# Splitting a 514-column product over two PSUM banks: 512 and 2 columns where there were two times 257

## The chip, the cores and the metric

The kernel runs on one core of one Trainium2 chip. A core has five engines that run side by side and meet at semaphores: TensorE (matmuls, out of SBUF into PSUM; the profile shows the matmuls as PE and the loads of their stationary operand as PEld), VectorE (DVE), ScalarE (ACT), GpSimd (POOL, here mostly the issue of indirect transfers) and SyncE (SP, the issue of the plain ones). The metric is the device time of one execution in microseconds. A float32 bank of PSUM holds 512 columns on each of 128 partitions in this kernel, so 514 columns need two banks.

## What is computed

The input `x` is (32, 512, 1024): a batch, 512 channels, 1024 nodes. Two layers, each with a residual and a layer norm over the last axis:

```python
# layer 0: attention over the nodes, in each batch
q = einsum('c,bcn->bn', wq, x);  k = einsum('c,bcn->bn', wk, x)
scores = q[:, None, :] + k[:, :, None]
scores = where(scores > 0, scores, 0.01 * scores)
att = softmax(scores, axis=-1)
agg = einsum('bcn,bmn->bcm', x, att)
x = layernorm(x + relu(einsum('oc,bcm->bom', adj, agg) + bm[None, :, None]))
# layer 1: a product with the elementwise square of adj
x = layernorm(x + einsum('bnf,nm->bmf', x, adj * adj) + bias)
```

The score of a pair depends on a sum q + k alone, through a function with one bend at zero. Once the nodes are sorted by q, the nodes on either side of the bend are a head and a tail of the sorted list, so the softmax's sums over 1024 nodes become two running sums, one from each end, each with its own exponential weight.

## The kernel before

**Data of a batch.** `adj @ x` comes first (`product`, L306 to L313): for each of 8 groups of 128 nodes four float32 matmuls of 128x128 weights by 512 columns, into one PSUM bank `z_ps`, copied to SBUF by ScalarE (`zt`, L316). Each node's row has 514 columns: 512 products, a one (whose running sum gives the softmax's denominator), and the node's own q. GpSimd scatters the rows in the order of q to DRAM (`scatter`, L324), and SyncE loads them back so that each of 128 partitions holds 8 neighbours of the sorted list (`sums_load`, L343).

**Running sums and carries.** VectorE runs along the 8 rows of every partition, upwards (`up`, L353) and downwards (`down`, L366), each step a scaled add of 514 or 513 columns. What a partition still lacks is the sum over all partitions before it (for the upward sums) or behind it (for the downward ones): the carry. It is a matmul of the partition totals, 128 partitions by 514 columns, with a triangle of ones, `before` or `behind` (`carry`, L374 to L382). As 514 columns don't fit one bank, the carry is two matmuls into two tiles of 257 columns, taken from the pool `p1` of four banks under the tag `m`, which the carries share with `z_ps`, `sum_ps`, `qk_ps` and `qk_tp`. `carry_copy` (L384 to L387) has ScalarE copy both tiles to SBUF: the upward carry into row 0 of the table, the downward one to a tile of its own. VectorE adds the carry to all rows (`spread_carry`, L402 to L405), and SyncE writes the table to DRAM.

**The rest of layer 0.** GpSimd gathers from the table one row for every node (`gather`, L432), ScalarE and VectorE mix the two halves with the exponential weights (`mix_scale` L454, `mix` L459), TensorE transposes the mix back to channels by nodes (`turn`, L482, eight 128-column transposes for each of four tiles of channels), VectorE adds the residual (L490), and ScalarE does statistics and norm.

**Layer 1.** The product with adj * adj is done by a Strassen-like scheme of quarters (`U`, `V`, `Y`, `Z`, `C11` and others; L540 and L575), seven products where eight would be plain, each of 512-column matmuls, preceded in places by a short bfloat16 matmul that brings the bias (L538).

**Order.** The order is written out by hand, as words of the form operation.batch.index: `head` for the first batches, `loop` once for each of the batches 12 to 25, `tail` for the last. Each engine executes its own share of that list in order. A round of the loop works on up to six batches in different stages: it loads one, ranks another, does sums and carries of a third, gathers and mixes a fourth, and so on. Around the carries a round reads

```
mx.-3.3 cu.-2 zc.-1.2 d.-2.5 s1.-4.2 t.-3.1 ... uc.-2
tu.-2.1 rt.-3 st.-4.3 cd.-2 z.-1.6 dc.-2 rce.-3 zc.-1.5 td.-2.0
```

`cu` and `cd` are the matmuls of the upward and the downward carry, `uc` and `dc` their copies, `t` the transposes, `tu` and `td` VectorE's adds of the carries, `rt` ScalarE's square root. On TensorE, `cu` stands ahead of a `t` and `cd` ahead of a `z`.

Of the kernel before, what the change touches and what calls it, by code (L numbers as in the profile page):

```python
# [34 lines left out]
F32 = mybir.dt.float32  # L35
# [7 lines left out]
P = 128  # L43
# [6 lines left out]
def adj_resnorm_kernel(  # L50
# [10 lines left out]
    nc = tc.nc  # L61
    B, C, N = x.shape
# [5 lines left out]
    ZR = C + 2  # L68
# [10 lines left out]
    p1 = ctx.enter_context(tc.tile_pool(name="p1", bufs=4, space=bass.MemoryType.PSUM))  # L79
# [21 lines left out]
    for h in range(2):  # L101
# [7 lines left out]
    before = const.tile([P, P], F32, name="before")  # L109
    nc.vector.memset(before, 1.0)  # L110
    nc.gpsimd.affine_select(
        before, before, pattern=[[1, P]], compare_op=ALU.is_gt, fill=0.0, base=0,
# [260 lines left out]

    def carry(b, m, v):  # L374

        half = ZR // 2
        ps = []
        for h in range(2):
            t = p1.tile([P, C], F32, tag="m", name=f"carry_ps_{b}_{h}_{m is before}")[:, 0:half]
            nc.tensor.matmul(t, m, v[:, h * half : (h + 1) * half], start=True, stop=True)  # L380
            ps.append(t)
        return ps  # L382

    def carry_copy(ps, to):  # L384
        half = ZR // 2
        for h, t in enumerate(ps):
            nc.scalar.copy(to[:, h * half : (h + 1) * half], t)  # L387

    def carry_up(b):
        st[b].cup = carry(b, before, st[b].end)  # L390

    def carry_up_copy(b):
        carry_copy(st[b].cup, st[b].tab[:, 0, 0:ZR])

    def carry_down(b):
        st[b].cdown = carry(b, behind, st[b].zs[:, 0, :])

    def carry_down_copy(b):
        st[b].carry = one.tile([P, ZR], F32, tag="carry", name=f"carry_{b}")
        carry_copy(st[b].cdown, st[b].carry)  # L400
# [562 lines left out]
```

## Time and profile before

| | before |
|---|---|
| median of three runs | 2062.61 us (2061.65 to 2064.26) |
| the profiled execution, in all | 2065.32 us |
| its span, first to last instruction | 2063.6 us |
| mean granted TensorE clock | 0.991 |
| TensorE busy, matmuls | 2004.7 us (97%), 6609 records |
| TensorE busy, weight loads | 956.7 us (46%), 6609 records |
| VectorE busy | 1674.9 us (81%) |
| ScalarE busy | 1496.3 us (73%) |
| GpSimd busy | 874.6 us (42%) |
| DMA | 541 MB, mean 262 GB/s |

A float32 matmul of the program shows up as two MATMUL records and two LDWEIGHTS records. In a row of groups, "x128" counts records, the first number after the bar is the time in which any of them ran, the second the mean length of one. Consecutive records overlap, since a matmul's way through the array is longer than the time for which it takes the input. Where a row says "idle", it is the idle time of that engine just before these instructions, and behind the arrow stands what ended it; "issue" means that nothing seen in the trace held it.

### The profile page before, as it was taken

Reading aid. Unit: us, or ns where it says so; the run is one execution under the profiler, and the core shown is the slowest. Engines: PE = TensorE matmul, PEld = TensorE weight load, DVE = VectorE, ACT = ScalarE, POOL = GpSimd, SP = SyncE. Lnnn points to the kernel's source line nnn. Section 1 sums busy time; section 2 is a strip of 40 time slices with the busy share of each in tenths; the row PEclk is TensorE's granted clock in tenths of the full one; section 3 lists DMA queues with packets and bytes.
Section 4 is the critical chain, followed back from the end, with each engine's and each line's share of the span. In section 5 each row is a group of like instructions: output and inputs, shape, how many; then the busy total and the mean of one; then the engine's idle time right before and its main releaser. Section 6 shows DMA issues by size and latency. Waiting matters only on the chain. (4 is left out here: it accounts for less than half of the span.)

```text
span 2063.6 us, 22066 instructions
## 1 busy us (share of the span) xinstructions
PE 2004.7 (97%) x6609; PEld 956.7 (46%) x6609; DVE 1674.9 (81%) x2778; ACT 1496.3 (73%) x2560; POOL 874.6 (42%) x1106
## 2 busy tenths in 40 slices
PE   8999999999999999999999999999999999999976
PEld 4444444444444444444444544444444444444432
DVE  6888898798877889887889888789778888789672
ACT  3566787678776777777777777777777777767566
POOL 4344543344343444443444443453444443443421
PEclk9999999999999999999999999999999999999988
DMA  5558776866667766667766767766677766677752
GB/s 226 212 222 312 275 287 266 306 264 257 271 245 291 307 255 246 271 266 292 306 241 250 273 268 296 290 249 258 255 276 306 276 244 268 245 269 273 286 204 82
DMA packets 137967, 541.04 MB, mean 262 GB/s; under 512 B 14404, under 2 KB 14416, under 8 KB 129656
## 3 DMA queue, kind: packets, MB, share of 16 engines
q1 hardware_dynamic: 80464, 337.47, 41.2%
q0 software_dynamic: 57344, 202.15, 26.0%
q8 instruction: 52, 0.85, 0.2%
q14 instruction: 67, 0.55, 0.1%
q10 hardware_dynamic: 40, 0.02, 0.0%
HBM read 270.29 MB, written 269.29 MB: 261 GB/s over the span
## 5 line engine op out<-in xcount | busy, mean ns | idle before, releaser
L310 PE MATMUL z_ps<-adj_t,x 128*128 128x512 f32 x2048 | 906.6, 593 | 0.4 <-ACT zt L316 0.4
L310 PEld LDWEIGHTS z_ps<-adj_t,x 128*128 128x128 f32 x2048 | 384.1, 190 | 448.0 <-issue 439.5
L324 POOL DMA_INDIRECT sorted_z<-zt,to x256 | 377.2, 1473 | 481.0 <-ACT zt L316 403.7
L432 POOL DMA_INDIRECT got<-table,of x256 | 262.2, 1024 | 209.6 <-issue 87.8
L271 DVE SCALAR_TENSOR_TENSOR junk_v<-qb,qkc,tie 128x1024 uint8<-128x1024 f32 x256 | 328.2, 1282 | 4.0
L284 ACT ACTIVATE junk_s<-qb,qkc 128x1024 bf16<-128x1024 f32 x256 | 293.9, 1148 | 18.9 <-DVE qb L261 17.0
L475 POOL TENSOR_SCALAR var<-var 128x1 f32<-128x1 f32 x128 | 46.3, 362 | 461.9 <-ACT junk L468 458.6
L454 ACT ACTIVATE got<-got,w 128x512 f32<-128x512 f32 x256 | 172.2, 713 | 64.2 <-DVE w L449 56.6
L316 ACT COPY zt<-z_ps 128x512 f32<-128x512 f32 x256 | 144.4, 577 | 68.4 <-PE z_ps L310 63.2
L459 DVE SCALAR_TENSOR_TENSOR got<-got,w 128x512 f32<-128x512 f32 x256 | 180.9, 745 | 10.9 <-ACT got L454 10.7
L490 DVE SCALAR_TENSOR_TENSOR x<-agg_ps,nbm,x 128x1024 f32<-128x1024 f32 x128 | 161.4, 1280 | 23.1 <-PE agg_ps L482 22.7
L372 DVE SCALAR_TENSOR_TENSOR tab<-tab,ac 128x513 f32<-128x513 f32 x224 | 168.0, 750 | 3.0
L631 ACT ACTIVATE g<-g,nb,var 128x1024 f32<-128x1024 f32 x128 | 157.8, 1238 | 11.8 <-POOL nb L625 11.8
L468 ACT ACTIVATE junk<-g,tot 128x1024 bf16<-128x1024 f32 x128 | 146.6, 1146 | 21.3 <-DVE g L595 16.8
L362 DVE SCALAR_TENSOR_TENSOR tab<-tab,ac 128x514 f32<-128x514 f32 x192 | 144.5, 752 | 16.9 <-ACT ac L348 11.7
L468 ACT ACTIVATE junk<-x,tot 128x1024 bf16<-128x1024 f32 x128 | 146.8, 1147 | 13.6 <-DVE x L490 8.3
L405 DVE TENSOR_TENSOR tab<-tab,carry 128x2052 f32<-128x2052 f32 x64 | 144.8, 2292 | 11.5 <-ACT carry L387 11.5
L540 PE MATMUL sum_ps<-x,adj 128*128 128x512 f32 x256 | 131.4, 637 | 16.3 <-ACT x L508 16.3
L482 PE MATMUL agg_ps<-ident,got 128*128 128x128 f32 x1024 | 133.4, 278 | 11.2 <-issue 4.7
L508 ACT ACTIVATE x<-x,var 128x1024 f32<-128x1024 f32 x128 | 138.5, 1149 | 0.7 <-DVE var L504 0.6
L601 DVE SCALAR_TENSOR_TENSOR g<-sum_ps,g 128x512 f32<-128x512 f32 x64 | 44.0, 687 | 111.8 <-ACT junk_s L284 75.3
L482 PEld LDWEIGHTS agg_ps<-ident,got 128*128 128x128 f32 x1024 | 115.2, 143 | 36.3 <-DVE x L490 12.2
(121 smaller groups left out, 2698.8 us busy)
## 6 DMA issues: line engine op xcount, KB each, us to landing
table<-tab SPq DMA_DIRECT2D x64, 2056.0 KB
tab<-sorted_z SPq DMA_DIRECT2D x64, 1028.0 KB
x<-in_x_dram SPq DMA_DIRECT2D x128, 512.0 KB
out_dram<-g SPq DMA_DIRECT2D x128, 512.0 KB
sorted_z<-zt,to POOLq DMA_INDIRECT x256
got<-table,of POOLq DMA_INDIRECT x256
adj_in<-in_adj_dram SPq DMA_DIRECT2D x1, 1024.0 KB
table<-end SPq DMA_DIRECT2D x32, 2.0 KB
```

What stands on the lines that cost most here:

```text
L271: nc.vector.scalar_tensor_tensor(junk, s.qb, s.q[:, j : j + 1], tie[:, at : at + N], ALU.subtract, ALU.is_gt, accum_out=s.rank[:, j : j + 1],)
L284: nc.scalar.activation(junk, s.qb, AF.Sign, bias=s.k[:, j : j + 1], accum_out=s.sign[:, j : j + 1])
L310: nc.tensor.matmul(s.z[j], xt[:, c, j * P : (j + 1) * P], adj_t[:, c, :], start=(c == 0), stop=(c == CT - 1),)
L324: nc.gpsimd.indirect_dma_start(out=sorted_z[b % 2][:, :], out_offset=bass.IndirectOffsetOnAxis(ap=s.to[:, j : j + 1], axis=0), in_=zt[:, j ...
L372: nc.vector.scalar_tensor_tensor(v, v, c, s.zs[:, j + 1, 0:D], ALU.mult, ALU.add)
L432: nc.gpsimd.indirect_dma_start(out=s.got[:, j, :], out_offset=None, in_=table[b % 2][:, :], in_offset=bass.IndirectOffsetOnAxis(ap=s.of[:, ...
L454: nc.scalar.activation(down, down, AF.Copy, scale=s.w[:, 1, j : j + 1])
L459: nc.vector.scalar_tensor_tensor(up, up, s.w[:, 0, j : j + 1], down, ALU.mult, ALU.add)
L468: nc.scalar.activation(junk, t, AF.Square, bias=v[0][:, i : i + 1], scale=-float(N), accum_out=v[1][:, i : i + 1],)
L482: nc.tensor.transpose(s.agg[o][:, j * P : (j + 1) * P], s.got[:, j, o * P : (o + 1) * P], ident)
L490: nc.vector.scalar_tensor_tensor(t[:, o, :], s.agg[o], nbm[:, o : o + 1], t[:, o, :], ALU.max, ALU.add, accum_out=s.v0[0][:, o : o + 1],)
L631: nc.scalar.activation(g, g, AF.Identity, bias=s.nb[:, m : m + 1], scale=s.v1[1][:, m : m + 1])
```

## The change

The carry's 514 columns are split where the first bank is full. The first matmul takes columns 0 to 511, the second the last two: column 512, the one's running sum, and column 513, q, which the table doesn't use. The copies are split in the same places. Both tiles come from the same pool and tag as before, there are as many matmuls, copies and banks as before, and the order of the words is unchanged.

```diff
     def carry(b, m, v):
 
-        half = ZR // 2
         ps = []
-        for h in range(2):
-            t = p1.tile([P, C], F32, tag="m", name=f"carry_ps_{b}_{h}_{m is before}")[:, 0:half]
-            nc.tensor.matmul(t, m, v[:, h * half : (h + 1) * half], start=True, stop=True)
+        for h, (lo, hi) in enumerate(((0, C), (C, ZR))):
+            t = p1.tile([P, C], F32, tag="m", name=f"carry_ps_{b}_{h}_{m is before}")[:, 0 : hi - lo]
+            nc.tensor.matmul(t, m, v[:, lo:hi], start=True, stop=True)
             ps.append(t)
         return ps
 
     def carry_copy(ps, to):
-        half = ZR // 2
-        for h, t in enumerate(ps):
-            nc.scalar.copy(to[:, h * half : (h + 1) * half], t)
+        for (lo, hi), t in zip(((0, C), (C, ZR)), ps):
+            nc.scalar.copy(to[:, lo:hi], t)
```

Here `P` is 128, `C` is 512 and `ZR` is 514.

## The prediction

> **What bounds the kernel now.** I read the page's busy times and slices first, then busy time by stretch, then the groups with their shapes kept apart, then the waits of TensorE, and last single instructions around carries in the timeline.
>
> ```profile
> PE 2004.7 (97%) x6609; PEld 956.7 (46%) x6609; DVE 1674.9 (81%) x2778; ACT 1496.3 (73%) x2560; POOL 874.6 (42%) x1106
> ...
> PE   8999999999999999999999999999999999999976
> ```
>
> TensorE is busy 97% of the span; VectorE, second, 81%. The slices put the missing 3% at both ends. The table of stretches makes this sharper (stretch, its length, then busy time of PE, PEld, DVE, ACT, POOL with counts, granted clock, DMA share, GB/s):
>
> ```profile
> 100.00:600.00 500.00, 491.34 (x1592) 232.48 (x1591) 422.44 (x707) 371.69 (x645) 218.98 (x267) 1.00 0.72 277
> 600.00:1100.00 500.00, 498.76 (x1655) 238.95 (x1654) 414.02 (x689) 374.25 (x641) 219.28 (x272) 1.00 0.69 270
> 1100.00:1600.00 500.00, 497.62 (x1653) 238.52 (x1652) 417.33 (x694) 376.15 (x644) 219.70 (x272) 1.00 0.69 271
> 1600.00:1950.00 350.00, 347.08 (x1141) 165.87 (x1140) 287.61 (x466) 256.17 (x440) 149.54 (x192) 1.00 0.69 267
> ```
>
> Between 600 and 1600 us TensorE stands still for 3.6 us of 1000 (1.24 and 2.38), at full granted clock (1.00), while no other engine is above 84%. In the loop, what TensorE issues is the time; what the others do counts only when TensorE waits for it. Among its waits, this one recurs in the middle, TensorE's transposes waiting for VectorE's mix (us in total, times, longest):
>
> ```profile
> PE agg_ps L482 <- DVE got L459: 4.5, 9, 1.0
> ```
>
> I come back to it. The groups that the change touches, and the large products to compare with (count | busy us, mean ns of one | idle before):
>
> ```profile
> L310 PE MATMUL z_ps<-adj_t,x 128*128 128x512 f32 x2048 | 906.6, 593 | 0.4 <-ACT zt L316 0.4
> ...
> L380 PE MATMUL carry_ps_False<-tab,behind 128*128 128x257 f32 x128 | 34.0, 388 | 0.4 <-ACT tab L387 0.4
> ...
> L387 ACT COPY carry<-carry_ps_False 128x257 f32<-128x257 f32 x64 | 21.3, 368 | 7.8 <-PE carry_ps_False L380 7.3
> ```
>
> The trace has two MATMUL and two LDWEIGHTS records for each float32 product: 128 records a side are 64 matmuls, two carries in each of 32 batches. "Mean ns of one" holds the way through the array; the pace is busy over count: 906.6/2048 = 443 ns for 512 columns with the ends of runs in it, 427 to 430 between two starts. The same row shows that TensorE waits only 0.4 us in all for the release of a PSUM bank by the copy to zt. Here is one carry of the loop, and what surrounds it:
>
> ```profile
> 1114.27 1.03 PE L380 MATMUL carry_ps_False<-tab,behind 128*128 128x257 f32 x4
> ...
> 1115.14 1.88 PE L310 MATMUL z_ps<-adj_t,x 128*128 128x512 f32 x4
> ...
> 1115.54 0.63 ACT L387 COPY carry<-carry_ps_False 128x257 f32<-128x257 f32 x2
> 1115.57 0.19 PEld L310 LDWEIGHTS z_ps<-adj_t,x 128*128 128x128 f32 x1 [0.24 <-issue]
> ...
> 1116.20 2.29 DVE L405 TENSOR_TENSOR tab<-tab,carry 128x2052 f32<-128x2052 f32 x1 [0.36 <-ACT carry L387]
> ```
>
> Four 257-column records run from 1114.27 to the start of z_ps at 1115.14: 0.87 us, 217 ns each. The first 512-column record starts at 1115.14, and the weight load seen at 1115.57, with the second, 0.43 later; ahead of it the weight path was free for 0.24. So a record of N columns takes the array about N/1.2 ns (214, 427), and the load of 190 ns on the next record's weights starts with each matmul and is gone before that matmul has streamed. VectorE starts adding the carry at 1116.20, 0.03 us after the second copy ends (1115.54 + 0.63).
>
> What an *uncovered* load costs is seen where TensorE had stood still, a matmul, then loads:
>
> ```profile
> 1721.70 0.70 PE L310 MATMUL z_ps<-adj_t,x 128*128 128x512 f32 x1 [0.38 <-ACT zt L316]
> ```
>
> ```profile
> 1720.62 0.30 PEld L380 LDWEIGHTS carry_ps_True<-end,before 128*128 128x128 f32 x2 [0.69 <-ACT g L608]
> 1721.69 0.30 PEld L310 LDWEIGHTS z_ps<-adj_t,x 128*128 128x128 f32 x2 [0.78 <-ACT zt L316]
> ```
>
> The second load starts 0.11 us after the first (0.30 less one load's 0.19), and the 512-column matmul takes 0.70 instead of its usual 0.59. Ten such loads between 200 and 1960 us give 107 to 109 ns. That is how long an uncovered 128x128 float32 load holds the array, not its whole 190. For the transposes it is less:
>
> ```profile
> 1101.83 0.33 PE L482 MATMUL agg_ps<-ident,got 128*128 128x128 f32 x1 [0.42 <-DVE got L459]
> ```
>
> 0.33 against 0.273 for most of this line's matmuls: 57 ns.
>
> **What the Trainium skill says.** "TensorE: Matmul & The Clock Gate", section LDWEIGHTS, prices a weight load by columns, P/1.2: 107 ns for 128, as the 0.11 above. The same page's "Step-by-step" says that a load is pulled ahead of running matmuls into the background weight buffer; the trace agrees, and shows it one load ahead: each starts with the matmul before its own. "Wait — 56ns, not 53.3ns?" gives a floor of about 25 ns between matmul starts however few columns; no run here shows so small a matmul. "ScalarE: Activation LUTs", section What ACT_TABLE_LOAD costs, gives 186 ns + 0.833 ns per element for an ACTIVATE with immediate operands; the trace's copies have about that slope (577 for the 512 columns of L316, 369 for 257: 208/255 = 0.816) on a smaller base.
>
> **The change, part by part.**
>
> *TensorE.* Removed are four records of 257 columns, 4 x 217.5 = 870 ns. Added are two of 512, 2 x 429 = 858 ns, and two of 2 columns. The columns are the same 514, so streaming changes by nothing (2 columns stream in under 5 ns), but the number of weight loads stays four, and what covers them goes. The load of the first small record hides under the second large one. The load of the second small record can start only with the first small record, and has nothing over it: 107 ns, which also swallows the 25 ns floor. The load of whatever comes next starts with the second small record: 107 ns before a float32 matmul, 58 before a transpose. So
> - before a product: 858 + 107 + 107 - 870 = +202 ns; this is the neighbour of 31 carries (30 z_ps, one sum_ps);
> - before a transpose (L482 27 times, L252 four, L236 once): 858 + 107 + 58 - 870 = +153 ns, 32 carries;
> - once the bias matmul L538 follows, whose own load was uncovered anyway: about +100 ns.
>
> 31 x 0.202 + 32 x 0.153 + 0.1 = 11.3 us of TensorE work. The small records aren't in this trace: below, 58 for each of the two loads (58 + 58 - 12 = 104 ns a carry, 6.7 us); above, the load's full 190 (368 ns, 23.6 us). I take 107, which is measured on this very kind of load, and keep both ends.
>
> *What absorbs some.* Where TensorE waits soon after a carry, the wait shrinks. By the timeline 14 of the 64 carries have such a wait within some 4 us behind them (the nine before L482, five others before 420 and after 1700 us): 14 x 0.16 = -2.2 us. Most of the loop's carries have none.
>
> *ScalarE.* Two copies of 257 (353 and 375 ns, the second starting 252 after the first: 627 in all) become one of 512 (577, pace some 470) and one of 2 (about 165 from the base 577 - 512 x 0.816, the page's price 188): 635 to 660. Nothing to speak of, under ScalarE's 25% of idle time; without that cover 64 x 0.03 = 2 us.
>
> *Latency of the carry.* The first product is complete 429 + 592 = 1.02 us after the carry's start, before 0.60. In the loop ScalarE comes to the copy 1.15 to 1.27 us after it (1115.54 - 1114.27), for it has the square root's table load and ACTIVATE ahead of it, so this hides, by only 0.13; and carry_up's copy comes 3 us later. Where ScalarE already waited for the product, some ten carries at the ends, the copies end about 0.26 us later (1.02 + 0.04 + 0.58 + 0.07 against 1.44). On the path to the end are one near the start and the last one at 1970.87, run at half clock: +0.5 us together. Behind these copies VectorE's table add and the table's write would be late.
>
> *PSUM.* Still two of four banks; the first is freed about 0.2 us later. Four banks are deep enough, as the 0.4 us says.
>
> Sum: 11.3 - 2.2 + 0.5 = +9.6 us. The profiled execution took 2065.32 (span 2063.6 and 1.7 around it), which gives 2074.9; it lay 2.7 above the median of the runs, so the median goes from 2062.61 to **2072.2**. A difference under 0.2% (4.1 us) can't be told from none.
>
> **Rivals.**
> - *A small record holds the array for the load's whole 190 ns* (or the short matmul's way through the array shows): 23.6 - 3.4 absorbed + 0.5, about 2083. For it: the record's 190, and that no case here has two uncovered loads with a matmul between. Against: after waits the next load starts 0.11 later every time.
> - *Not slower: loads run further ahead.* If the load of a small record's successor could be finished while the 512-column record streams, only streaming counts: 870 becomes 858 and a few ns, -0.6 us, 2062. The place is the second large record, 429 ns long and covering one load of 107; it decides if two or three loads fit under it. For it: the 32-column loads of L221 run four ahead, though each for another quarter of the array's columns. Against: the loads of full width begin 1 to 2 ns after the preceding matmul, and the 0.24 us that stay free under each large record are used by none.
> - *The waits swallow it.* TensorE stands still for 8.7 us from 100 to 600 and 6.5 more to 1950, enough for the sum if it lay in the right places; but it takes waits behind 45 of 64 carries (45 x 0.16 = 7.2) to bring the change under 4.1 us, and between 600 and 1600 six carries have one. About 2066.
>
> **Chances.** Forecast 0.80 (own range 2067 to 2080, its lower end the 58 ns bound: 6.7 less some 2 absorbed; its upper end some 150 ns a load); whole-load rival 0.08; loads further ahead or waits swallowing 0.12, of which 0.03 for a gain above 4.1 us through a path that I don't see. The range 2067 to 2080 leaves out 0.20. Slower 0.88, same 0.09, faster 0.03.
>
> **What would show it.** In the changed trace: L380 with 512- and 2-column forms, 128 records each; from a carry's first start to the next matmul's 1.07 us where z_ps follows, 1.02 before transposes, instead of 0.87; weight loads around the small matmuls 0.11 apart; VectorE's and ScalarE's busy times unchanged within 3 us; copies in the loop starting at the same distance from the carry. Each loop of about 62 us longer by 0.35. Wrong it would be if the small records' loads start early (then no change), if the distance to the next matmul is above 1.2 us (then the whole load counts), or if VectorE's wait for the carry's copy grows beyond 12 us to 20, a new wait in the loop.

## The result and the profile after

| | before | after |
|---|---|---|
| median, 7 runs each | 2062.83 us (2061.65 to 2066.96) | 2071.99 us (2069.96 to 2074.31) |
| ratio | | 1.0045, interval 1.0036 to 1.0055 |
| span of the profiled execution | 2063.6 us | 2071.2 us |
| TensorE busy | 2004.7 us | 2015.2 us |
| mean granted TensorE clock | 0.991 | 0.991 |

The change makes the kernel 9.2 us slower by the medians (7.4 to 11.3 by the 95% interval of the ratio). The page's busy times after the change:

```profile
PE 2015.2 (97%) x6609; PEld 947.3 (46%) x6609; DVE 1675.3 (81%) x2778; ACT 1497.1 (72%) x2560; POOL 871.4 (42%) x1106
```

TensorE has 10.5 us more work at the same number of instructions; VectorE and ScalarE moved by less than 1 us. Busy times by stretch, with the columns that the prediction explains:

```profile
100.00:600.00 500.00, 490.55 (x1580) 228.48 (x1579) 417.58 (x697) 366.63 (x638) 220.48 (x268) 0.99 0.71 276
600.00:1100.00 500.00, 499.26 (x1650) 235.53 (x1649) 415.94 (x694) 376.49 (x642) 218.38 (x272) 1.00 0.69 270
1100.00:1600.00 500.00, 500.00 (x1653) 236.18 (x1652) 415.07 (x692) 377.10 (x643) 214.24 (x272) 1.00 0.69 270
1600.00:1950.00 350.00, 347.74 (x1140) 164.09 (x1139) 286.72 (x463) 257.94 (x440) 146.04 (x187) 1.00 0.68 263
```

TensorE has still less idle time in the loop: 0.7 us between 600 and 1600, none of it behind 1100. A carry of the loop in the timeline:

```profile
1120.70 1.14 PE L379 MATMUL carry_ps_False<-tab,behind 128*128 128x512 f32 x4
...
1121.56 0.19 PEld L379 LDWEIGHTS carry_ps_False<-tab,behind 128*128 128x128 f32 x1 [0.24 <-issue]
...
1121.67 0.30 PEld L310 LDWEIGHTS z_ps<-adj_t,x 128*128 128x128 f32 x2
1121.70 1.96 PE L310 MATMUL z_ps<-adj_t,x 128*128 128x512 f32 x4
1121.76 0.65 ACT L385 COPY carry<-carry_ps_False 128x512 f32<-128x512 f32 x2
...
1122.44 2.30 DVE L403 TENSOR_TENSOR tab<-tab,carry 128x2052 f32<-128x2052 f32 x1 [0.59 <-ACT carry L385]
```

The carry starts at 1120.70. The last of the carry's four weight loads, that of the second 2-column record, starts at 1121.56; the next load, the first of z_ps, at 1121.67, and the one behind it 0.11 later again ("x2" in 0.30 us). So the loads around the small records stand 0.11 apart, and all that streams meanwhile is 2 columns at a time. The next z_ps matmul is listed at 1121.70, but its input begins only with the load at 1121.78 (1121.67 + 0.11). From the carry's start to there are 1.08 us, where it was 0.87. On ScalarE, the first copy starts at 1121.76, 1.06 us after the carry, as soon as the first product is complete, and VectorE's add follows the second copy at 1122.44.

The groups by shape, of the downward carry; first VectorE's row before the change, for its wait, then the rows after it:

```profile
L405 DVE TENSOR_TENSOR tab<-tab,carry 128x2052 f32<-128x2052 f32 x64 | 144.8, 2292 | 11.5 <-ACT carry L387 11.5
```

```profile
L403 DVE TENSOR_TENSOR tab<-tab,carry 128x2052 f32<-128x2052 f32 x64 | 144.9, 2292 | 16.8 <-ACT carry L385 16.8
...
L379 PE MATMUL carry_ps_False<-tab,behind 128*128 128x512 f32 x64 | 32.8, 593 | 0.4 <-ACT tab L385 0.4
...
L385 ACT COPY carry<-carry_ps_False 128x512 f32<-128x512 f32 x32 | 18.6, 581 | 11.4 <-PE carry_ps_False L379 9.6
...
L379 PE MATMUL carry_ps_False<-tab,behind 128*128 128x2 f32 x64 | 9.0, 209 | 0.0
...
L385 ACT COPY carry<-carry_ps_False 128x2 f32<-128x2 f32 x32 | 5.3, 166 | 0.0
```

In the loop a pair of copies takes 0.65 us from start to end, where it took 0.63 (two groups that overlap, so 18.6 and 5.3 can't be added up), and VectorE's wait for them grew from 11.5 to 16.8 us. TensorE's wait for the mix, 4.5 us in nine places before, is now

```profile
PE agg_ps L480 <- DVE got L457: 1.9, 5, 0.6
```

Two theories stand. **Uncovered loads**: the loads around each small record cost TensorE 0.21 us before a product and 0.165 before a transpose, and TensorE bounds the kernel. **Late copies**: the first product is complete 0.43 us later, so the copies can end later, and VectorE, which shows 5.3 us more of waiting, passes that on. The experiments take these apart.

### The profile page after: what moved, and what is told of

Same layout as the page of the kernel before. It is cut to its first block, busy times and chain, and to the rows that moved or that the text cites. A ratio compares the mean times of both kernels' runs of the same rounds, so it can differ in the third digit from the quotient of the medians.

```text
span 2071.2 us, 22066 instructions
## 1 busy us (share of the span) xinstructions
PE 2015.2 (97%) x6609; PEld 947.3 (46%) x6609; DVE 1675.3 (81%) x2778; ACT 1497.1 (72%) x2560; POOL 871.4 (42%) x1106
## 5 line engine op out<-in xcount | busy, mean ns | idle before, releaser
L403 DVE TENSOR_TENSOR tab<-tab,carry 128x2052 f32<-128x2052 f32 x64 | 144.9, 2292 | 16.8 <-ACT carry L385 16.8
L403 DVE TENSOR_TENSOR tab<-tab 128x1539 f32<-128x1539 f32 (+1 forms) x64 | 129.3, 2024 | 0.6 <-ACT tab L385 0.6
```

Of the source, the lines that this page charges most:

```text
L403: nc.vector.tensor_tensor(v, v, c, ALU.add)
```

## The experiments

"Before" in a comparison is the kernel before, timed beside the run; in brackets behind a ratio stands its 95% interval. Distances are from a carry's first record to the second record behind the carry, medians from the traces: the second, since the start that is listed for the first lies ahead of its load. Before, they are 1.299 us where z_ps stands behind and 0.978 where L482 does; after, 1.514 and 1.143: +0.215 and +0.165.

### Small products outside the carries

```diff
         s.z[j] = p1.tile([P, C], F32, tag="m", name=f"z_ps_{b}_{j}")
+        if j in (2, 6):
+            nc.tensor.matmul(s.z[j][:, 0:2], before, xt[:, 0, 0:2], start=True, stop=True)
```

> The carries stay at two times 257 columns. Ahead of two of the eight z_ps groups of each batch (the ones that stand next to the carries on TensorE) one more float32 product of 2 columns is put, 64 in all, into the bank that the group then overwrites; the result is unchanged and no copy waits for it later than before by more than its own 0.2 us. Uncovered loads (my theory): each costs 0.21 to 0.22 us of TensorE, 13.9 us in all, of which 2 to 5 are absorbed by waits as with the change: 2072 to 2075, with VectorE's wait for the carries' copies at 10 to 13 us as before. Late copies (the rival: the change costs because its first product is complete 0.43 us later and its copies end later): the carries are untouched, so 2063 within 2.

Measured: 2070.51 against 2062.8 us, ratio 1.0041 (1.0028 to 1.0054). TensorE around one of those that stand right behind a downward carry:

```profile
1118.72 1.03 PE L382 MATMUL carry_ps_False<-tab,behind 128*128 128x257 f32 x4
1119.59 0.28 PE L310 MATMUL z_ps<-x,before 128*128 128x2 f32 x2
1119.73 3.68 PE L312 MATMUL z_ps<-adj_t,x 128*128 128x512 f32 x8
```

From the first small record to the second z_ps record are 0.652 us (median), of which 0.429 are z_ps: each costs 0.223 us, 64 of them 14.3. VectorE's wait for the carries' copies is 12.3 us, near the 11.5 before the change. So small products alone, with untouched carries, give a loss of the change's size. The time fell short of the expectation by 1.5 us: by the medians 6.6 us were absorbed, where I had put 2 to 5. By the interval, a loss of 5.8 to 11.1 us, it may be 3 to 8, so this miss isn't clear of the noise, and what absorbed it isn't shown.

### The change without its small product

```diff
-        for h, (lo, hi) in enumerate(((0, C), (C, ZR))):
+        for h, (lo, hi) in enumerate(((0, C),)):
 ...
-    def carry_copy(ps, to):
-        for (lo, hi), t in zip(((0, C), (C, ZR)), ps):
-            nc.scalar.copy(to[:, lo:hi], t)
+    def carry_copy(ps, to, v):
+        nc.scalar.copy(to[:, 0:C], ps[0])
+        nc.scalar.copy(to[:, C:ZR], v[:, C:ZR])
```

`v` is the input of the carry's products, `s.end` or `s.zs[:, 0, :]`, passed along by the two callers.

> The change with its product of 2 columns left out; ScalarE still makes the second copy, but takes the two columns from the uncarried totals in SBUF, so the denominators are wrong. The 512-column product and its copy are as late as in the change. Uncovered loads: only 858 instead of 870 ns of TensorE remain in each carry, so 2062 within 1.5 and each carry 12 ns shorter than before. Late copies: the first product is complete as late as in the change and VectorE's wait for the carries' copies stays at about 17 us, so most of the 9 us stays: 2069 to 2072.

Measured: 2063.24 against 2062.8 us, ratio 1.0001 (0.9993 to 1.0009); the distances are 1.289 and 0.967, 10 and 11 ns below before. VectorE's wait for the copies stayed up:

```profile
L403 DVE TENSOR_TENSOR tab<-tab,carry 128x2052 f32<-128x2052 f32 x64 | 144.9, 2292 | 17.1 <-ACT carry L385 17.1
```

17.1 us of waiting, as much as in the change, and no loss. This is the run that decides: the late first product and VectorE's longer wait are there, and they cost nothing that these runs can tell; the small product is what costs. The interval leaves the late copies 1.9 us, and 0.7 more for the 10 to 11 ns by which each carry is shorter here, of the change's 9.2. The run also takes one PSUM bank less for each carry; the next one takes as many as the change and loses nothing either, so the banks are not it.

### The split at 384 and at 448

```diff
-        for h, (lo, hi) in enumerate(((0, C), (C, ZR))):
+        for h, (lo, hi) in enumerate(((0, 384), (384, ZR))):
```

The same in `carry_copy`, and likewise with 448.

> The same edit as the change, with the split at 384: 384 and 130 columns. Uncovered loads: a record of 130 columns streams for 108 to 111 ns, as long as a weight load holds the array, so nothing is uncovered: 870 ns a carry within 10, and 2063 within 1.5. Late copies: the first product is complete 0.21 us later than before, half of the change's 0.43, so about half of its loss: 2067 to 2068.

> The split at 448: 448 and 66 columns. Uncovered loads: a record of 66 columns streams for 57 ns and leaves some 55 ns of each load uncovered: two loads before a float32 product (+0.10 us, 31 carries), one before a transpose, whose own load takes only 58 (+0.05, 32 carries), 5.0 us in all and 1 to 2 of them absorbed: 2065.5 to 2067. Late copies: the first product is complete 0.32 us later, three quarters of the change's 0.43: 2069 to 2070.

Measured: 384 gives 2063.9 us (1.0003, 0.9994 to 1.0012), 448 gives 2066.39 us (1.0020, 1.0013 to 1.0027). One downward carry of each on TensorE, first 384, then 448:

```profile
1113.36 1.03 PE L379 MATMUL carry_ps_False<-tab,behind 128*128 128x384 f32 x4
1114.23 3.60 PE L310 MATMUL z_ps<-adj_t,x 128*128 128x512 f32 x8
```

```profile
1115.88 1.09 PE L379 MATMUL carry_ps_False<-tab,behind 128*128 128x448 f32 x4
1116.81 3.65 PE L310 MATMUL z_ps<-adj_t,x 128*128 128x512 f32 x8
```

From the carry to z_ps are 0.87 us at 384 and, with the load still to come, 0.93 listed at 448. The distances are 1.300 and 0.977 at 384 (before: 1.299, 0.978), 1.407 and 1.036 at 448 (+0.108 and +0.058). So a record of 130 columns, which streams about as long as a load holds the array, costs nothing, uneven as the split is; at 66 columns half of each load shows. The late copies would have asked for 2067 and 2069.

### One direction at a time

```diff
+    def cut(m):
+        k = C if m is before else ZR // 2
+        return (0, k), (k, ZR)
```

`carry` and `carry_copy` take their bounds from `cut(m)`; for the other direction `behind` stands for `before`.

> 512 and 2 columns for the upward carry alone; the downward one stays at two times 257. Behind 26 of these 32 stand transposes. Uncovered loads: 26 x 0.165 + 5 x 0.215 + about 0.1 = 5.5 us of TensorE, of which the waits of the transposes just behind absorb the larger part of what the whole change loses to waits, some 2: 2066 to 2067.5. If instead what is absorbed does not depend on what stands behind the carry, it is 46% of the whole change's 9: 2067. Late copies: ScalarE comes to this copy 3 us after the carry, so nothing: 2063.

> 512 and 2 columns for the downward carry alone. Behind 25 of these 32 stands a z_ps product. Uncovered loads: 25 x 0.215 + 6 x 0.165 + 0.1 = 6.5 us of TensorE, little of it absorbed: 2068 to 2069.5, and with the upward one's the 9 of the whole change within 2. Late copies: this is the carry that VectorE waits for, so it should hold all of the change's loss: 2072.

Measured, with before at 2061.66 us: upward alone 2065.21 (1.0015, 1.0008 to 1.0021), downward alone 2068.34 (1.0033, 1.0020 to 1.0046). That is +3.6 and +6.7 us by the medians, 10.3 together; the whole change measured 9.2. By the distances TensorE's work grew by 5.6 and 6.4 us (the trace has 25 transposes and 7 products behind the upward carries, and 7, 24 and the bias behind the downward ones; the expectations had one of them on the other side). The upward carry, with transposes and their waits behind it, gives back some 2 us, 1.3 to 4.0 by the interval; for the downward one nothing can be told. Late copies fail again: they allowed the upward carry no loss. VectorE's row in the run with the downward change,

```profile
L407 DVE TENSOR_TENSOR tab<-tab,carry 128x2052 f32<-128x2052 f32 x64 | 144.9, 2293 | 16.2 <-ACT carry L389 16.2
```

shows that the longer wait, 16.2 us, comes with the downward carry; in the run with the upward change it is 11.8.

### The small product first

```diff
-        for h, (lo, hi) in enumerate(((0, C), (C, ZR))):
+        for h, (lo, hi) in enumerate(((C, ZR), (0, C))):
```

> The change with the 2 columns ahead of the 512, in products and copies. Uncovered loads: the second small record's load and the first large one's are uncovered, both of the float32 kind, 111 ns each, whatever stands behind: from a carry's start to the next matmul 1.08 us, also before transposes (the change: 1.03 there), 64 x 0.21 = 13.4 us of TensorE instead of 12; 2072 to 2075. Late copies: the second product is complete 1.67 us after the start instead of 1.14, the copy of 512 columns ends 0.5 us later than in the change: 2078 or more.

Measured: 2072.98 against 2061.66 us, ratio 1.0054 (1.0041 to 1.0067). An upward carry with the transposes behind it, in the change and then here:

```profile
1107.07 1.14 PE L379 MATMUL carry_ps_True<-end,before 128*128 128x512 f32 x4
1108.07 1.07 PE L480 MATMUL agg_ps<-ident,got 128*128 128x128 f32 x8
```

```profile
1108.14 1.25 PE L379 MATMUL carry_ps_True<-end,before 128*128 128x2 f32 x4
1109.22 1.91 PE L480 MATMUL agg_ps<-ident,got 128*128 128x128 f32 x16
```

1.00 and 1.08 us from the carry to the transposes' listed start; the distances to the second transpose are 1.143 and 1.191, and before z_ps 1.514 and 1.512. So the load that shows is the one *behind* a small record, and its price is that of its own kind. VectorE's wait for the copies went to 21.1 us, without the 2078 that late copies would give.

### More rows for the bias matmul

If loads that nothing covers cost that much, the kernel before has others. In front of some groups stands a bfloat16 matmul that brings the bias from 6 partitions, 128 in all:

```profile
1119.45 3.60 PE L310 MATMUL z_ps<-adj_t,x 128*128 128x512 f32 x8
1122.98 0.38 PE L538 MATMUL sum_ps<-bias_p,first 6*128 6x512 bf16 x1
1123.29 1.98 PE L540 MATMUL sum_ps<-x,adj 128*128 128x512 f32 x4
```

The 8 z_ps records start at 1119.45 and should be through at 1122.88 (8 x 0.429); the bias starts at 1122.98, and the next product 0.31 later, though 512 bfloat16 columns stream in 0.215 (the distance to the following record once its load is covered, below). About 0.2 us of two loads show in these starts each time.

```diff
-    bias_p = const.tile([6, H], BF16, name="bias_p")
-    first_0 = const.tile([6, P], BF16, name="first_0")
-    first_10 = const.tile([6, P], BF16, name="first_10")
+    bias_p = const.tile([P, H], BF16, name="bias_p")
+    first_0 = const.tile([P, P], BF16, name="first_0")
+    first_10 = const.tile([P, P], BF16, name="first_10")
 ...
-        nc.vector.tensor_copy(first_0, own[:, 4:5].broadcast_to([6, P]))
-        nc.vector.memset(first_10, 1.0)
+        for v in (bias_p, first_0, first_10):
+            nc.vector.memset(v, 0.0)
+        nc.vector.tensor_copy(first_0[0:6, :], own[:, 4:5].broadcast_to([6, P]))
+        nc.vector.memset(first_10[0:6, :], 1.0)
 ...
-        nc.vector.tensor_copy(bias_p, done)
+        nc.vector.tensor_copy(bias_p[0:6, :], done)
```

> The kernel before, with the bias operands of L538 padded by zeros from 6 to 128 rows; all else as before. The 128 bias matmuls stand 0.524 us behind a record that streams for 0.429, and the record behind them follows 0.314 after their own 0.215, so each leaves some 0.2 us of two loads uncovered. If that comes from the 6 rows (a load for part of the rows isn't pulled ahead, nor is the next one), both loads go under cover: 128 x 0.195 = 25 us less TensorE work, 2038 to 2046 as other engines' waits show up. If it comes from the change of type between float32 and bfloat16: 2063 within 2.

Measured: 2051.49 against 2061.66 us, ratio 0.9941 (0.9927 to 0.9956).

```profile
1116.29 3.60 PE L312 MATMUL z_ps<-adj_t,x 128*128 128x512 f32 x8
1119.72 0.38 PE L540 MATMUL sum_ps<-bias_p,first 128*128 128x512 bf16 x1
1119.94 3.81 PE L542 MATMUL sum_ps<-x,adj 128*128 128x512 f32 x8
```

From the eight z_ps to the bias are now 3.43 us, eight times 0.429, and 0.22 to the product behind it: both loads are covered, and the type still changes there, so it was the 6 rows. Both operands were padded; whether the 6 rows of the load or those of the columns that stream matter is not separated. (The last row takes 3.81 us for eight products, not 3.60, as one more bias matmul stands among them whose record is missing. The trace has 96 of the 128; around 29 of the other 32 the neighbours stand 0.645 apart, which is 0.429 and 0.216.)

The expectation's 0.195 is too small. It counts two distances, which went from 0.525 to 0.429 and from 0.314 to 0.216; but the start listed for the first product behind the bias lies ahead of its load here too, and from it to the second record are 0.533 us before and 0.429 now. In all that is 0.298 a bias, and 128 x 0.298 = 38 us less TensorE work. Only 10 of them reached the time (16 in the repeat below). The loop gained nearly all of its share: the 16 rounds between the 10th and the 26th downward carry take 980.1 us, against 996.8 before and 991.5 in the run split at 384, whose TensorE work is that of before; 64 x 0.298 is 19. What lies ahead of these rounds gained nothing, nor did what lies behind, with 32 bias matmuls each: the 10th downward carry starts at 622.4 us (before 616.0, at 384 617.7). Two things are seen. At 233 and at 421 us the granted clock is at half for 3.4 us each, and again at 1838 for 6.8 us; before, it is full at these places. At half clock 3.4 us hold at most 1.7 us of work, so this takes up to 7 us of the execution shown here, which at 2056.04 us is the slowest of its kind (mean clock 0.986; in the repeat 0.989). And TensorE waits longer for the mix:

```profile
PE agg_ps L484 <- DVE got L461: 11.0, 9, 2.2
```

11.0 us where it was 4.5 (7.4 in the repeat). What else holds up the two ends, and whether the waits bring about the half clock, is not shown.

### The change on top of that

The same padding with the change's carries, beside the padded kernel once more.

> The kernel with the bias operands padded to 128 rows once more, as the base of the next run: 2051 within 3, carries at two times 257.

> The padded kernel with the change on top. Its carries take TensorE the same 12 us more. If what is absorbed grows with the waits that TensorE has (about 37 us between 100 and 1950 where the kernel before has 15), clearly more than the 3 of the change is absorbed, and this is 3 to 7 us above the padded kernel of the same call. If the exposed loads cost the same wherever TensorE is over 95% busy, it is 9 above, as before.

Measured side by side (before: 2065.09 us): padded 2049.1 (0.9928, 0.9915 to 0.9941), padded with the change 2059.2 (0.9975, 0.9966 to 0.9983). The change costs 10.1 us by the medians; from the two ratios 0.0047 with some 0.0015 of uncertainty, 6.6 to 12.8 us. The first alternative is the less likely, though its upper end isn't excluded. In the traces the same 16 rounds take 984.8 us with the change and 978.6 without; these 6.2 us are the whole price of 32 carries, 16 x 0.38 = 6.1. So more waits elsewhere did not shelter the carries. The padded kernel with even carries is the fastest one here.

## Why the prediction was right

The time forecast was 2072.2 us, the measured 2071.99, with the mechanism that was forecast. That the two lie this close is luck in part: the work was put 0.7 us too low, what is absorbed 0.6 too low, and 0.5 was set down for the ends that can't be seen, so the misses nearly cancel. Its steps one by one:

**TensorE bounds the loop.** Right. Work put on TensorE alone (small products at z_ps) lengthened the time, and a later first product alone (the change without its small product) did not, as far as the interval tells.

**What a load costs when nothing covers it.** Predicted 107 and 58 ns, +202 ns before a product and +153 before a transpose, 11.3 us in all. Measured +215 and +165. The sum with these is 31 x 0.215 + 32 x 0.165 + 0.1 = 12.0 us: the term was sized 6% too small. Loads around small records stand 111 ns apart (in the first experiment 652 - 429 = 223 for two), 2 to 4 more than those that follow a wait; what the remaining few nanoseconds are was not taken apart.

**What absorbs some.** Predicted 14 waits shrinking by 0.16 each, 2.2 us. The medians leave 12.0 - 9.2 = 2.8 us in all, 0.7 to 4.6 by the interval, so the size is near, but the picture was too simple. In the two profiled executions the nine waits for the mix did not shrink by 0.16 each: 4.5 us became 1.9, some vanishing whole. That is partly the executions' own: the split at 384, with TensorE work unchanged, also shows 1.9 us in its profile, an execution 2.2 us below its median. The sign "each loop longer by 0.35" is hidden by the same thing: the 16 rounds take 996.8 us before and 997.9 after, but 991.5 at 384, and against those the change adds 6.4 us, 0.40 a round. So the difference of the two profiles' spans, 7.6 us, says less than the medians. With one direction at a time, the upward carries gave back about 2 of 5.6 us and the downward ones nothing measurable, as their neighbours suggested.

**ScalarE.** Right: 577 and 165 ns were expected for the copies; the rows show 581 and 166.

**Latency of the carry.** The loop's copies were to stay hidden by 0.13 us. They did not, and one of the prediction's own signs of being wrong came: VectorE's wait for the copies grew beyond 12 us, to 16.8. In 13 of the 17 downward carries between 600 and 1650 us ScalarE's square root now ends 0.93 to 0.94 us after the carry's start (before, 1.24 or later in all of them), so its copy waits for the product until 1.06. Measured from the carry's start the copies even end a little earlier than before, 1.71 against 1.78 us (medians); VectorE waits longer because it is ready at 1.15 instead of 1.46 and the copies, held by the product, can't follow that far. More work on TensorE is not needed to shift the two engines: the split at 384 has none, and there too the root ends at 0.94 in 12 of 17 and VectorE is ready at 1.15; with its product complete earlier, the copies end at 1.50 and the wait is 12.2 us in all. Why both engines come later in the trace of the kernel before stays open. The 0.5 us set down for the ends can't be seen either: the run with the late copies and without small products measured +0.4 us, with an uncertainty of 1.7. So the step missed the wait, though its price, near nothing, was right. That VectorE catches up elsewhere in the round, as TensorE bounds it, is how I read this, and is not shown.

**The rivals.** That a small record holds the array for a load's whole 190 ns is refuted by the 0.11 between loads. That loads run further ahead is refuted by the same rows: around the carries no load started ahead of the matmul before its own. That waits swallow the change was worth about 3 us and not 7.

## What to carry to other kernels

A float32 product of 2 columns costs TensorE the two weight loads that its records can't cover, 0.165 to 0.223 us here. Columns moved from a wide product to a narrow one were free where each record streamed as long as a load holds the array (at 130 columns, not at 66; nothing in between was tried). Before splitting by bank, count the records and ask what stands over each load, also over that of the next instruction. Where TensorE is the bound, look in its timeline for every place where two matmul starts are further apart than the first one streams: here that led to 128 bias matmuls with 0.3 us each.

## What was not expected

The weight load of a matmul on 6 partitions, and the load behind it, lie open in this kernel; the same matmul with zeros up to 128 partitions has both covered, 0.298 us less for each such matmul, and the kernel is 0.6 to 0.7% faster for it. Also unexpected was how little VectorE's waits mean here: 5 us more of them, right at the place of the change, came with no loss that the runs can tell.
